# Adder convolutions: a pair of maxima added by DMA, and four channels in one written order

## The chip, the cores and the metric

The kernel runs on one core of a Trainium2 chip. The metric is device time in microseconds (us) of one execution of the whole program. The kernel before the change took 21,893.29 us in the median of three runs (21,889.71 to 21,903.57).

A core has several engines that run their own instruction lists in order and wait for each other through semaphores: TensorE (PE, matrix products into PSUM), VectorE (DVE), ScalarE (ACT), GpSimd (POOL) and SyncE (SP, which here issues DMAs). Sixteen DMA engines move data.

## The reference

The program is a chain of four layers on a tensor of 4 images, 128 channels and 64 x 64 points, all in float32: self-attention over the points (layer 0), two pairs of "shift" and "adder" convolution with batch norm (layer 1), a local attention block with an MLP (layer 2), and a selective scan (layer 3). Only layer 1 is changed. Its adder convolution is an L1 distance between each 3 x 3 patch and each output channel's weights:

```python
patches = lax.conv_general_dilated_patches(x, filter_shape=(K, K), ...)
def per_channel(wc):
    return -jnp.sum(jnp.abs(p - wc[None, :, None]), axis=1)
out = lax.map(per_channel, wf)
```

For one image and one output channel this is a sum of |p - w| over 128 input channels and 9 taps at 4096 points. There are 4 images, 128 output channels and two such convolutions: 1,024 image-channels, each with 9 taps of 128 x 4096 elements.

## The kernel before

`layer1` calls `shift_adder` twice (tags a1 and a2). The shift convolution of image b writes its result with a border of zeros into a buffer `pb` in SBUF; the adder convolution reads nine shifted views of it. Input channels lie on the 128 partitions, the 4096 points along each row.

The absolute value of a tap is made in one of two ways. ScalarE computes |p - w| directly (`absolute`, line 423, weights as the bias). VectorE computes max(p, w) (`maximum`, line 430), because |p - w| = 2 max(p, w) - p - w; the terms in p and w are put in at the end, from the sums of the window over the input channels (`sums_of_p`) and the sums of the weights (`wsum`). A third form, `plus_maximum` (line 434), adds a maximum onto a finished tile in one VectorE instruction. When it adds onto an absolute value, ScalarE has made that one with scale 0.5 (`HALF_TAP`), so the factor 2 fits both.

Each finished tile of 128 x 4096 is a *stream*: PE sums it over the partitions with eight matmuls of 512 columns (`gather`, line 381) against a vector of -1 or -2 that stands in the column of the channel (`pick`), into two PSUM banks that collect 32 output channels (a chunk). A float32 matmul has two records in the profile, so a stream has sixteen.

A channel has four activations (taps 7, 4, 5, 6), four maxima (taps 0 to 3) and one added maximum (tap 8 onto tap 7): eight streams. In every fourth channel of the first three images (`extra`) the last maximum is added onto the one before it, which leaves seven streams, and three steps of other work (`beside`) are put on PE: the window sums of this image and the shift convolution of the next. Every 32 channels `evacuate` empties the two banks.

The order of the work is that of the Python loop over channels (line 416) as the framework's scheduler lays it out. Engines run ahead as far as buffers allow: `ap` has four tiles for absolute values, `dp` three for maxima. GpSimd only clears borders (lines 84, 85 and 331), and SyncE issues all DMAs of this layer.

Of the kernel before, what the change touches and what calls it, by code (L numbers as in the profile page):

```python
# [16 lines left out]
P = 128  # L17
B = 4
# [11 lines left out]
DVE_TAPS = (0, 1, 2, 3)  # L30
ACT_TAPS = (4, 5, 6)
HALF_TAP = 7
MAX_TAP = 8
# [248 lines left out]
def shift_adder(tc, cm, load, wqs, w_add, stats, y_d, tag):  # L282
# [5 lines left out]

    nc = tc.nc
    NC = P // 32  # L290
    with ExitStack() as ctx:
# [4 lines left out]
        for t, scale in [(HALF_TAP, -0.5)] + [(t, -1.0) for t in ACT_TAPS]:  # L296
            wn[t] = cp.tile([P, P], F32, name=f"{tag}wn{t}")
            nc.vector.tensor_scalar(wn[t], wa[:, t, :], scale, None, ALU.mult)

        pick = {}  # L300
        for v in (-1.0, -2.0):
            pick[v] = cp.tile([P, 63], F32, name=f"{tag}pick{int(-v)}")
            nc.vector.memset(pick[v], 0.0)
            nc.vector.memset(pick[v][:, 31:32], v)

        xin_pool = ctx.enter_context(tc.tile_pool(name=f"{tag}x", bufs=3))
        pb_pool = ctx.enter_context(tc.tile_pool(name=f"{tag}p", bufs=2))
        dp = ctx.enter_context(tc.tile_pool(name=f"{tag}d", bufs=3))
        ap = ctx.enter_context(tc.tile_pool(name=f"{tag}a", bufs=4))
# [6 lines left out]
        sum_taps = DVE_TAPS + (MAX_TAP,)  # L316
        pw = ps_c.tile([P, NC], F32, tag="cv", name=f"{tag}pw")
        for c in range(NC):
            for g in range(4):
                for i, t in enumerate(sum_taps):  # L320
                    nc.tensor.matmul(
                        pw[32 * g : 32 * g + 32, c : c + 1], wa[:, t, 32 * c : 32 * c + 32], cm.one_col,
                        start=(i == 0), stop=(i == len(sum_taps) - 1), skip_group_check=True,
                    )
# [3 lines left out]
        def fetch(b, k):  # L328

            t = xin_pool.tile([P, RB + 2, HP], F32, tag="xin", name=f"{tag}xin{b}_{k}")  # L330
            nc.gpsimd.memset(t[:, :, 0:HP:HP - 1], 0.0)
            if k == 0:
                nc.gpsimd.memset(t[:, 0, 1 : 1 + W], 0.0)
            if k == NB - 1:
                nc.gpsimd.memset(t[:, RB + 1, 1 : 1 + W], 0.0)
            lo, hi = max(RB * k - 1, 0), min(RB * (k + 1) + 1, H)
            at = lo - (RB * k - 1)
            load(b, lo, hi, t[:, at : at + hi - lo, 1 : 1 + W])
            return t

        def convolution(b, pb):

            xin = fetch(b, 0)
            for k in range(NB):
                here, xin = xin, fetch(b, k + 1) if k < NB - 1 else None
                pc = ps_c.tile([P, BK], F32, tag="cv", name=f"{tag}pc{b}_{k}")
                for t in range(TAPS):
                    y, x = divmod(t, 3)
                    nc.tensor.matmul(
                        pc, wqs[:, t, :], here[:, y : y + RB, x : x + W],  # L350
                        start=(t == 0), stop=(t == TAPS - 1),
                    )
                    if t == TAPS - 1:
                        nc.vector.tensor_copy(pb[:, 1 + RB * k : 1 + RB * (k + 1), 1 : 1 + W], rows(pc))  # L354
                    yield

        def padded(b):
            t = pb_pool.tile([P, HP, HP], F32, tag="pb", name=f"{tag}pb{b}")
            clear_border(nc, t)
            return t  # L360

        def sums_of_p(b, pb, sp):

            for k in range(2):
                pc = ps_c.tile([P, BK], F32, tag="cv", name=f"{tag}sp{b}_{k}")
                for i, t in enumerate(sum_taps):
                    y, x = divmod(t, 3)
                    for g in range(4):
                        r = RB * (4 * k + g) + y
                        nc.tensor.matmul(  # L370
                            pc[32 * g : 32 * g + 32, :], cm.ones[:, 0:32], pb[:, r : r + RB, x : x + W],
                            start=(i == 0), stop=(i == len(sum_taps) - 1), skip_group_check=True,
                        )
                    yield
                nc.vector.tensor_copy(sp[:, k, :], pc)

        def gather(pa, jj, v, d, first=False):

            for k in range(2):
                for g in range(4):  # L380
                    nc.tensor.matmul(  # L381
                        pa[k][32 * g : 32 * g + 32, :],
                        pick[v][:, 31 - jj : 63 - jj],
                        d[:, bass.ts(4 * k + g, BK)],
                        start=first, stop=False, skip_group_check=True,
                    )

        def evacuate(b, c, pa, sp):
            for k in range(2):
                o = ep.tile([P, BK], F32, tag="ev", name=f"{tag}ev{b}_{c}_{k}")  # L390
                nc.vector.scalar_tensor_tensor(o, pa[k], wsum[:, c : c + 1], sp[:, k, :], ALU.add, ALU.add)
                nc.vector.bn_stats(stats[:, c, 2 * b + k, :], o)
                to = y_d[b, 32 * c : 32 * c + 32, :].rearrange("j (k g w) -> k g j w", k=2, g=4)
                nc.sync.dma_start(to[k], o)
# [11 lines left out]
        done, late = None, []  # L406
        for b in range(B):
            pb = pb_of[b]

            def view(t):  # L410
                y, x = divmod(t, 3)
                return pb[:, y : y + H, x : x + W]

            sp_of[b] = sp_pool.tile([P, 2, BK], F32, tag="sp", bufs=2, name=f"{tag}sps{b}")
            steps = beside(b, pb_of)
            for co in range(P):
                c, jj = divmod(co, 32)
                name = f"{tag}_{b}_{co}_"

                def absolute(t):  # L420
                    at = ap.tile([P, N], F32, tag="ab", name=f"a{name}{t}")
                    half = t == HALF_TAP
                    nc.scalar.activation(  # L423
                        rows(at), view(t), AF.Abs, bias=wn[t][:, co : co + 1], scale=0.5 if half else 1.0
                    )
                    return at

                def maximum(t):
                    dt = dp.tile([P, N], F32, tag="ad", name=f"d{name}{t}")
                    nc.vector.tensor_scalar(rows(dt), view(t), wa[:, t, co : co + 1], None, ALU.max)  # L430
                    return dt

                def plus_maximum(at, t):
                    nc.vector.scalar_tensor_tensor(  # L434
                        rows(at), view(t), wa[:, t, co : co + 1], rows(at), ALU.max, ALU.add
                    )

                if jj == 0:
                    pa = [
                        ps_a.tile([P, BK], F32, tag=f"pa{k}", name=f"{tag}pa{b}_{c}_{k}") for k in range(2)  # L440
                    ]


                extra = b < B - 1 and co % 4 == 1
                ah = absolute(HALF_TAP)
                d = maximum(DVE_TAPS[0])
                for g in late:
                    gather(*g)
                gather(pa, jj, -2.0, d, first=(jj == 0))
                if done and jj == 0:  # L450
                    evacuate(*done)
                d = maximum(DVE_TAPS[1])
                gather(pa, jj, -2.0, d)
                a = absolute(ACT_TAPS[0])
                gather(pa, jj, -1.0, a)
                a = absolute(ACT_TAPS[1])
                plus_maximum(ah, MAX_TAP)
                gather(pa, jj, -2.0, ah)
                gather(pa, jj, -1.0, a)
                if extra or b == B - 1:  # L460
                    for _ in range(3 if extra else 1):
                        next(steps, None)
                d = maximum(DVE_TAPS[2])
                if extra:
                    plus_maximum(d, DVE_TAPS[3])
                    a = absolute(ACT_TAPS[2])
                    late = [(pa, jj, -1.0, a), (pa, jj, -2.0, d)]
                else:
                    gather(pa, jj, -2.0, d)
                    a = absolute(ACT_TAPS[2])  # L470
                    d = maximum(DVE_TAPS[3])
                    gather(pa, jj, -2.0, d)
                    late = [(pa, jj, -1.0, a)]
                if jj == 31:
                    done = (b, c, pa, sp_of[b])
            for _ in steps:
                pass
        for g in late:
            gather(*g)
        evacuate(*done)  # L480


@with_exitstack
def layer1(ctx, tc, cm, w_shift1, w_add1, g1, b1, w_shift2, w_add2, g2, b2, x1d, y1d, y2d, stats_d):
# [26 lines left out]
    def plain(b, lo, hi, t):  # L511
        nc.sync.dma_start(t, rows(x1d[b])[:, lo:hi, :])

# [4 lines left out]
    def normed(b, lo, hi, t):  # L518
        nc.sync.dma_start(t, rows(y1d[b])[:, lo:hi, :])
        nc.vector.tensor_scalar(t, t, mean1, sc1, ALU.subtract, ALU.mult)  # L520
        nc.scalar.activation(t, t, AF.Relu, bias=vec["b1"])
# [872 lines left out]
```

## Time and profile before

| What | Before |
|---|---|
| median of three runs | 21,893.29 us |
| profiled execution, own time | 21,893.77 us |
| its span, first to last instruction | 21,891.9 us |
| busy: PE / DVE / ACT / POOL | 20,152.1 / 19,729.2 / 18,548.7 / 3,775.6 us |
| a1, first to last activation start | 2083.6 to 9540.2 us |
| a2, first to last activation start | 9640.0 to 17,103.6 us |
| DMA share in the adder stages | 0.01 |

The page lists groups of instructions as: line, engine, operation, output tile <- input tiles, shapes, count | busy us, mean ns of one | idle time of the engine just before them and what ended it. Records of one engine overlap slightly, and the ends of matmuls are modelled, so the distance between starts is a better measure of pace than a duration. `da` are maxima, `aa` absolute values, `a1pa` and `a2pa` the PSUM banks. In answers on one line of the code, three numbers with slashes are the minimum, median and maximum duration in ns.

### The profile page before, as it was taken

Reading aid. Unit: us, or ns where it says so; the run is one execution under the profiler, and the core shown is the slowest. Engines: PE = TensorE matmul, PEld = TensorE weight load, DVE = VectorE, ACT = ScalarE, POOL = GpSimd, SP = SyncE. Lnnn points to the kernel's source line nnn. Section 1 sums busy time; section 2 is a strip of 40 time slices with the busy share of each in tenths; the row PEclk is TensorE's granted clock in tenths of the full one; section 3 lists DMA queues with packets and bytes.
Section 4 is the critical chain, followed back from the end, with each engine's and each line's share of the span. In section 5 each row is a group of like instructions: output and inputs, shape, how many; then the busy total and the mean of one; then the engine's idle time right before and its main releaser. Section 6 shows DMA issues by size and latency. Waiting matters only on the chain.

```text
span 21891.9 us, 327596 instructions
## 1 busy us (share of the span) xinstructions
PE 20152.1 (92%) x144108; PEld 6497.4 (30%) x144108; DVE 19729.2 (90%) x9928; ACT 18548.7 (85%) x9373; POOL 3775.6 (17%) x1774
## 2 busy tenths in 40 slices
PE   9998999999999999999999999999999656779998
PEld 4443222222222232232222222222322222223333
DVE  7787999999999999989999999999999766589998
ACT  5665999999999999989999999999999422556766
POOL 5664000000000000000000000000000000179998
PEclk9999999999999999999999999999999777689999
DMA  0000000000000000000000000000000000279997
GB/s 12 13 5 14 3 4 4 3 5 4 3 4 3 4 3 2 2 8 4 4 3 4 4 4 2 4 3 3 2 2 2 33 0 5 109 224 246 254 255 220
DMA packets 279019, 811.94 MB, mean 37 GB/s; under 512 B 131212, under 2 KB 132116, under 8 KB 207444
## 3 DMA queue, kind: packets, MB, share of 16 engines
q1 hardware_dynamic: 277012, 782.60, 12.5%
q8 instruction: 1127, 18.46, 0.3%
q10 hardware_dynamic: 576, 8.39, 0.1%
q14 instruction: 304, 2.49, 0.0%
HBM read 662.02 MB, written 128.78 MB: 36 GB/s over the span
## 4 chain that ended last, share of the span: by engine, by line
ACT 29%; PE 25%; DVE 24%; issue 16%; DMA 3%; POOL 2%; SPq 1%; DVEq 0%; ACTq 0%; POOLq 0%
ACT aa L423 27%; DVE da L430 11%; PE a1pa L381 6%; PE pe L154 4%; PE pav L197 4%; PE a2pa L381 3%; DVE h L1043 3%; DVE da L434 3%; DVE aa L434 3%; DVE g L713 1%; PE mg L1058 1%; DMA du<-du_d 1%; PE pd L698 1%; POOL dbu L1022 1%; DMA dl<-delta_d 1%
## 5 line engine op out<-in xcount | busy, mean ns | idle before, releaser
L423 ACT ACTIVATE aa<-a1pb,a1wn 128x4096 f32<-128x4096 f32 x2048 | 7411.6, 3711 | 179.2 <-DVE a1pb L354 130.5
L423 ACT ACTIVATE aa<-a2pb,a2wn 128x4096 f32<-128x4096 f32 x2048 | 7410.6, 3712 | 45.4 <-PE a2pa L381 41.5
L430 DVE TENSOR_SCALAR da<-a2pb,a2wa 128x4096 f32<-128x4096 f32 x1952 | 4470.3, 2347 | 0.2
L430 DVE TENSOR_SCALAR da<-a1pb,a1wa 128x4096 f32<-128x4096 f32 x1952 | 4469.5, 2347 | 0.7 <-PE a1pa L381 0.6
L381 PE MATMUL a2pa<-da,a2pick 128*32 128x512 f32 x31232 | 3617.3, 594 | 254.8 <-DVE da L430 252.0
L381 PE MATMUL a1pa<-da,a1pick 128*32 128x512 f32 x31232 | 3615.2, 594 | 253.5 <-DVE da L430 250.8
L381 PE MATMUL a2pa<-aa,a2pick 128*32 128x512 f32 x32768 | 3714.1, 593 | 4.8 <-ACT aa L423 3.3
L381 PE MATMUL a1pa<-aa,a1pick 128*32 128x512 f32 x32768 | 3712.5, 592 | 4.9 <-ACT aa L423 3.3
L434 DVE SCALAR_TENSOR_TENSOR aa<-a1pb,a1wa,aa 128x4096 f32<-128x4096 f32 x512 | 2295.1, 4483 | 282.2 <-ACT aa L423 278.0
L434 DVE SCALAR_TENSOR_TENSOR aa<-a2pb,a2wa,aa 128x4096 f32<-128x4096 f32 x512 | 2295.2, 4483 | 278.3 <-ACT aa L423 274.7
L1058 PE MATMUL mg<-h,ident 128*128 128x512 f32 x4096 | 1955.7, 615 | 204.4 <-ACT m L1067 168.6
L1043 DVE TENSOR_TENSOR_SCAN h<-da,h,dbu 128x1024 f32<-128x1024 f32 x768 | 1804.4, 2350 | 125.6 <-ACT da L1029 35.9
L381 PEld LDWEIGHTS a2pa<-aa,a2pick 128*32 128x32 f32 x32768 | 1069.1, 110 | 2464.8 <-issue 2397.0
L381 PEld LDWEIGHTS a1pa<-aa,a1pick 128*32 128x32 f32 x32768 | 1068.9, 110 | 2463.4 <-issue 2400.0
L381 PEld LDWEIGHTS a2pa<-da,a2pick 128*32 128x32 f32 x31232 | 987.3, 110 | 2706.9 <-issue 2053.2
L381 PEld LDWEIGHTS a1pa<-da,a1pick 128*32 128x32 f32 x31232 | 987.3, 110 | 2704.8 <-issue 2053.9
L191 POOL TENSOR_TENSOR ssum<-ssum,et 128x512 f32<-128x512 f32 x960 | 1228.8, 1280 | 233.4 <-ACT et L186 166.6
L1022 POOL TENSOR_TENSOR dbu<-du,B 128x2048 f32<-128x2048 f32 x256 | 1157.1, 4533 | 104.1 <-DMA du<-du_d 49.6
L1071 POOL TENSOR_TENSOR m<-m,C 128x2048 f32<-128x2048 f32 x256 | 1156.6, 4529 | 93.5 <-ACT m L1067 79.9
L1058 PEld LDWEIGHTS mg<-h,ident 128*128 128x128 f32 x4096 | 724.7, 191 | 1437.7 <-ACT m L1067 699.2
L156 ACT COPY et<-pe 128x512 f32<-128x512 f32 x1024 | 595.5, 582 | 592.2 <-PE pe L154 575.4
L154 PE MATMUL pe<-q,k 128*128 128x512 f32 x2048 | 1051.1, 596 | 8.7 <-DVE mx L164 8.1
(273 smaller groups left out, 13587.0 us busy)
## 6 DMA issues: line engine op xcount, KB each, us to landing
dl<-delta_d SPq DMA_DIRECT2D x256, 512.0 KB
dl<-delta_d SPq DMA_DIRECT2D x512, 256.0 KB
du<-du_d SPq DMA_DIRECT2D x256, 512.0 KB
du<-du_d SPq DMA_DIRECT2D x512, 256.0 KB
xs_d<-xs SPq DMA_DIRECT2D x8, 2048.0 KB
sz_d<-sz SPq DMA_DIRECT2D x64, 256.0 KB
delta_d<-dv SPq DMA_DIRECT2D x32, 512.0 KB
du_d<-du SPq DMA_DIRECT2D x32, 512.0 KB
```

Source lines behind the costliest of these rows:

```text
L154: nc.tensor.matmul(pe, k[:, bass.ts(j, P)], unit[u, "q"], start=True, stop=True)
L156: nc.scalar.copy(et, pe)
L191: nc.gpsimd.tensor_tensor(unit[u, "sum"], unit[u, "sum"], at, ALU.add)
L197: nc.tensor.matmul(unit[u, "av"], image[u // NB][2][:, j, :], at, start=(j == 0), stop=(j == NJ - 1))
L381: nc.tensor.matmul(pa[k][32 * g : 32 * g + 32, :], pick[v][:, 31 - jj : 63 - jj], d[:, bass.ts(4 * k + g, BK)], start=first, stop=False, s ...
L423: nc.scalar.activation(rows(at), view(t), AF.Abs, bias=wn[t][:, co : co + 1], scale=0.5 if half else 1.0)
L430: nc.vector.tensor_scalar(rows(dt), view(t), wa[:, t, co : co + 1], None, ALU.max)
L434: nc.vector.scalar_tensor_tensor(rows(at), view(t), wa[:, t, co : co + 1], rows(at), ALU.max, ALU.add)
L1022: then(nc.gpsimd.tensor_tensor(t, du, by_states(tiles[n][0], 0, h), ALU.mult))
L1043: then(nc.vector.tensor_tensor_scan(t[:, cols][:, s], da[:, s], st[n, "dbu", h][:, cols][:, s], 0.0 if e % 4 == 0 else st["last"], ALU.mul ...
L1058: then(nc.tensor.matmul(pm, cm.ident, st[n, way, h][:, bass.ts(k, BK)], start=(way == 0), stop=(way == 1)))
L1071: then(nc.gpsimd.tensor_tensor(m, m, by_states(tiles[n][0], 1, h), ALU.mult))
```

## The change

Four consecutive channels become one pattern with three kinds of channel.

- In every channel taps 0 and 1 are a *pair*: VectorE makes both maxima in two halves of 2048 points, and a DMA on GpSimd's queue adds one onto the other in SBUF (`accum_op=ALU.add`). The half sums are half streams; together the two halves are one stream.
- Channel 0 of four: three more maxima (taps 2, 3, 4) and four absolute values (5 to 8).
- Channels 1 and 3: two more maxima (2, 3), four absolute values, and tap 4 added onto one of them, made with scale 0.5.
- Channel 2: four more maxima (2 to 5), three absolute values (6 to 8).

That is 8, 7, 8 and 7 streams. For four channels: 15 activations, 11 full maxima, 16 half maxima, 2 added maxima, 8 adding DMAs of 1 MB and 30 streams. Tap 5 is a maximum only in channel 2 of four, so its part of the window sums and weight sums is taken through `third` and `w_third`, which hold ones and weights in those channels alone; the window sums now have six taps.

The order is written out as a string, `ORDER`, for four channels; the number ahead of a letter is the channel (-1 is the last channel of the four before). Capital letters make something (P pair, M maximum, A absolute value, S added maximum), the same letters small sum it on PE, and C stands for three steps of the other work and the evacuation. `keep_in_program_order` pins every instruction of the stage on its engine's list to that order. Absolute values get three buffers, full maxima two, half maxima six. The shift convolution fetches its input two blocks ahead instead of one.

```diff
-DVE_TAPS = (0, 1, 2, 3)
-ACT_TAPS = (4, 5, 6)
-HALF_TAP = 7
-MAX_TAP = 8
+PAIR_TAPS = (0, 1)
+MAX_TAPS = (2, 3, 4, 5)
+ADDED_TAP = 4
+ABS_TAPS = {0: (5, 6, 7, 8), 1: (5, 6, 7, 8), 2: (6, 7, 8), 3: (5, 6, 7, 8)}
+HALF = {1: 2, 3: 1}
+ORDER = """
+    -1p0 0P0 -1m0 0M0 0a0 0A2 0M1 0a1 -1p1 0A3 0m0 0P1 0m1 0M2 1A0 0a2 0a3 1P1 1M1 1A1 0m2 0p0 1a0 1P0
+    1A2 1m1 1M0 0p1 1a1 1A3 1S2 1m0 1p1 2A0 1a3 2M2 1a2 2M3 1p0 2A1 2m2 2M0 2a0 2A2 2m3 2a1 2P0 3A0 2M1
+    2m0 2a2 3A1 2P1 2m1 3a0 3P0 3A2 3S1 3C0 3A3 2p0 3a2 3P1 3a1 3M1 2p1 4A0 3a3 3M0 3m1 4A1
+""".split()
...
-        dp = ctx.enter_context(tc.tile_pool(name=f"{tag}d", bufs=3))
-        ap = ctx.enter_context(tc.tile_pool(name=f"{tag}a", bufs=4))
+        mp = ctx.enter_context(tc.tile_pool(name=f"{tag}m", bufs=6))
+        dp = ctx.enter_context(tc.tile_pool(name=f"{tag}d", bufs=2))
+        ap = ctx.enter_context(tc.tile_pool(name=f"{tag}a", bufs=3))
...
+        def pair(n, h):
+            ms = []
+            for t in PAIR_TAPS:
+                mt = mp.tile([P, HL], F32, tag="am", name=f"m{tag}_{n}_{t}_{h}")
+                v = view(n, t, h * H // 2, (h + 1) * H // 2)
+                then(nc.vector.tensor_scalar(rows(mt), v, weight(n, t), None, ALU.max))
+                ms.append(mt)
+            then(nc.gpsimd.dma_start(ms[1], ms[0], accum_op=ALU.add))
+            streams[n, "p", h] = (-2.0, ms[1], (h,))
...
+        for n in range(0, B * P, 4):
+            b, co = divmod(n, P)
+            if co == 0:
+                sp_of[b] = sp_pool.tile([P, 2, BK], F32, tag="sp", bufs=2, name=f"{tag}sps{b}")
+                steps = beside(b, pb_of)
+            for at, kind, i in map(parsed, ORDER):
+                m = n + at
+                if kind == "C":
+                    for _ in range(3):
+                        next(steps, None)
...
+                elif kind in make:
+                    if m < B * P:
+                        begin(m, kind, i)
+                else:
+                    summed(m, kind, i)
```

## The prediction

> **What bounds the kernel now.** I read the page first for where the time lies, then busy time by stretch, then the order in time inside one stretch, because shares over the whole span mix stages. The page's group list puts the two adder convolutions (a1, a2) on top:
>
> ```profile
> span 21891.9 us, 327596 instructions
> ...
> L423 ACT ACTIVATE aa<-a1pb,a1wn 128x4096 f32<-128x4096 f32 x2048 | 7411.6, 3711 | 179.2 <-DVE a1pb L354 130.5
> ...
> L430 DVE TENSOR_SCALAR da<-a2pb,a2wa 128x4096 f32<-128x4096 f32 x1952 | 4470.3, 2347 | 0.2
> ...
> L381 PE MATMUL a2pa<-da,a2pick 128*32 128x512 f32 x31232 | 3617.3, 594 | 254.8 <-DVE da L430 252.0
> ...
> L434 DVE SCALAR_TENSOR_TENSOR aa<-a1pb,a1wa,aa 128x4096 f32<-128x4096 f32 x512 | 2295.1, 4483 | 282.2 <-ACT aa L423 278.0
> ```
>
> By line 423's own answer a1 runs from 2083.6 to 9540.2 us and a2 from 9640.0 to 17103.6 (starts of the first and last activation). With the last one's 3.7 us that is 7460 and 7467 us for 512 image-channels each: 14.57 and 14.58 us a channel, 1,024 channels, 68% of the span. Two stretches of 500 us inside a1 (columns: stretch, length, then busy us and instructions of each engine, clock, DMA share, GB/s):
>
> ```profile
> 5900.00:6400.00 500.00, 482.68 (x4306) 145.74 (x4302) 486.05 (x179) 496.51 (x138) 0.26 (x2) 1.00 0.01 4
> 6400.00:6900.00 500.00, 485.82 (x4312) 143.27 (x4308) 483.73 (x179) 495.90 (x138) 0.25 (x2) 1.00 0.01 4
> ```
>
> ScalarE (fourth busy figure) is at 99%; PE and VectorE at 97%. ScalarE sets the pace and the others are close behind. Record durations overlap a little, so I take intervals between starts from the timeline:
>
> ```profile
> 5999.80 36.19 ACT L423 ACTIVATE aa<-a1pb,a1wn 128x4096 f32<-128x4096 f32 x10
> 6000.71 9.13 DVE L430 TENSOR_SCALAR da<-a1pb,a1wa 128x4096 f32<-128x4096 f32 x4
> 6004.85 5.33 PE L381 MATMUL a1pa<-aa,a1pick 128*32 128x512 f32 x48
> 6010.00 3.62 PE L381 MATMUL a1pa<-da,a1pick 128*32 128x512 f32 x32
> ```
>
> Activation: (36.19-3.71)/9 = 3.61 us. Maximum: (9.13-2.35)/3 = 2.26. Added maximum: 4.39 (start 6021.95, next start 6026.34). PE: 5.15 us from start to start over 48 records = 0.107 us, and a stream has 8 matmuls of two records, so 1.72 us. A half-size maximum (128x2048) exists elsewhere, line 711 at 1284 ns mean, so an interval near 1.20.
>
> [...]
>
> ```profile
> L212 DVE TENSOR_SCALAR o<-o,bv,g x32: 536/1580/1586, 158.1 to 1978.3; 128x512 f32<-128x512 f32 x32
> ...
> L331 POOL MEMSET a1xin<- x32: 123/126/3117, 2009.2 to 6902.7; 128x20 f32 x32
> ```
>
> (minimum/median/maximum ns). L212 took 0.54 us with GpSimd idle and 1.58 when a GpSimd addition of 1.26 us had begun with it. The GpSimd memset of 126 ns took 3.12 us once: it began at 5376.56 inside the first of two back-to-back maxima (5374.99 to 5379.60) and ended only after the second. Back-to-back maxima do not let GpSimd in between; inside an added maximum (two SBUF inputs) memsets took their 0.13 us.
>
> **The change, part by part, for four channels.**
> ScalarE: 16 activations become 15: 15 x 3.61 = 54.2 us, 13.54 a channel (before 14.44, and 14.57 measured: 0.13 above its floor).
> PE: 31.25 streams on average (7.75 a channel in three images, 8 in the last) become 30: 30 x 1.72 / 4 = 12.88, plus the next image's convolution, 144 records of about 0.47 us over 128 channels = 0.54, plus the window sums, now six taps, 96 x 0.107/128 = 0.08. Sum 13.50 (before 14.0).
> VectorE: 11 maxima x 2.26 = 24.9; 16 half maxima x 1.20 = 19.2; 2 added maxima x 4.39 = 8.8; 52.9/4 = 13.22, plus evacuations and copies, about 0.12: 13.34 (before about 13.95).
> GpSimd and DMA, new: eight additions of 1 MB each. A row of 8 KB is one packet, and the shortest 8 KB packets in the trace took 0.309 us; eight rows an engine read twice are 4.9 us, 8 x 4.9 = 39.6 us of a period near 55: 72% of DMA engines that are at 1% now. [...] What hides it: between a pair's making and its sum the written order puts 8.5, 6.5, 6, 6, 4, 4.5, 5 and 7 PE streams, the three of 4 to 5 with 2.8 us of convolution as well: 9.7 to 14.6 us, and 6.9 where no convolution is left (the last image). The six half buffers hold three pairs, and the shortest stretch of VectorE work before a pair's buffer returns is about 11 us. [...] beyond it PE waits, its queue is in order, and all later streams wait, then the two buffers of the full maxima, then VectorE.
> Fetches two ahead, other constants, `third`: some tens of small operations a layer, at nothing. They lie beside the same stream work; uncovered they are a few us.
>
> Sum: the floors are 13.54, 13.50, 13.34. The old excess was 0.13 with the next engine 0.4 behind; with three engines within 0.2 us and one fixed order I take 0.20: 13.74, 0.83 less than 14.57. Times 1,024 = 850. The profiled execution's own time is 21,893.8 us (span 21,891.9) and the median of runs 21,893.3, so both give **21,045 us**.
>
> The unknown is the descriptor writing. Lower bound nothing (Pool is idle, 0.26 us busy in 500). Upper bound: a lock held as by a GpSimd addition, 1.27 us, eight times, would put VectorE at 13.34 + 2 x 1.27 = 15.9. I take at most 0.2 us each, which VectorE's slack absorbs, and keep both ends.
>
> **Rivals.**
> *Part of the gain*: GpSimd gets in, holding VectorE 0.3 to 0.5 us a DMA. VectorE then has 13.94 to 14.34 plus 0.1: 21,390 to 21,800. For it: L212. Equal to before at about 0.6 us a DMA.
> *Slower[...]*: from the second half pair of the fourth channel (3P1) to 1M0 stand twelve tokens, five pairs and seven full maxima[...]: 5 x 2.4 + 7 x 2.26 = 27.8 us. If they run back to back, the descriptors of pairs made early in that stretch wait as the memset did, past the 10 to 14 us of cover. PE then stops, buffers fill, VectorE stops, and only then GpSimd gets in. [...] It decides from 3.3 us exposed per four channels (4 x 0.83). Against it: semaphore waits break such stretches, and a gap is all GpSimd needs.
> *Slower, through the DMA's rate*: eight transfers must fit in 58 us to equal before, 7.3 us each. At 8.2 us (2 MB of reads at the 255 GB/s of the scan stage) the DMA alone needs 16.4 us a channel: 23,770. Against it: 131,212 of the span's 279,019 packets are under 512 B, and these are 8 KB.
> *No change*: gain and stalls cancel, 21,850 to 21,940. That the edit is not made is excluded: the built program has 1,920 activations a layer where it had 2,048, and 1,024 adding DMAs.
>
> **How the numbers follow.** Likeliest, cover holds: 0.45, between 20,900 (excess 0.06) and 21,250. Part of the gain, to 21,850: 0.13. Cancelled: 0.03. [...] 0.39 in all, of which about 0.22 below 22,900. The range 20,900 to 22,900 leaves out 0.17 above and 0.03 below. Within 0.2%, about what a measurement tells from none, counts as same.
>
> **What would show it.** Right: ScalarE again at 98 to 99% in a1, one channel per 13.7 us, PE's waits on the pair's DMA short, half maxima at 1.28 us, landings under 10 us. [...] half or full maxima lengthened beyond 2.35, or VectorE idle on DMA semaphores and PE on pair streams, landings of 12 us and more with long GpSimd waits. Rate: DMA share near 1 in these stages. What would make me wrong: descriptors that cannot be written under maxima, or adding rows slower than two reads.

## The result and the profile after

The changed kernel takes 21,815.2 us in the median of seven runs (21,793.3 to 21,843.5), the kernel before 21,894.9 beside it: a ratio of 0.9964, 95% interval 0.9952 to 0.9976. It is faster by 80 us, 0.4%, where 850 were forecast. The profiled execution answers as follows. First the page: the span, the chain that ended last, groups of instructions (busy us, mean ns | idle time ahead of the group and what ended it), and the DMA's time to landing.

```profile
span 21809.7 us, 323448 instructions
...
DMA ma<-ma 26%; PE a2pa L424 11%; PE a1pa L424 11%; DVE ma L478 7%; DVE da L469 6%; PE pe L163 4%; PE pav L206 4%; DVE h L1092 3%; DVE g L762 1%; DMA du<-du_d 1%; PE mg L1107 1%; PE pd L747 1%; DMA dl<-delta_d 1%; POOL dbu L1071 1%; DVE aa L461 1%
...
L455 ACT ACTIVATE aa<-a1pb,a1wn 128x4096 f32<-128x4096 f32 x1920 | 6987.3, 3713 | 567.2 <-PE a1pa L424 431.0
...
L469 DVE TENSOR_SCALAR da<-a1pb,a1wa 128x4096 f32<-128x4096 f32 x1408 | 3275.0, 2348 | 293.1 <-PE a1pa L424 292.6
...
L478 DVE TENSOR_SCALAR ma<-a1pb,a1wa 128x2048 f32<-128x2048 f32 x2048 | 2545.0, 1280 | 267.8 <-DMA ma<-ma 266.4
...
L424 PE MATMUL a1pa<-ma,a1pick 128*32 128x512 f32 x8192 | 1090.7, 605 | 334.0 <-DMA ma<-ma 331.7
...
ma<-ma POOLq DMA_DIRECT2D x2048, 1024.0 KB, 9.3
```

The instructions have the durations that the prediction gave them: maxima 2348 ns, half maxima 1280 ns, neither lengthened. What is new is idle time on every engine of these stages, and one cause at its head: PE waits for the adding DMA ahead of the pair sums, ScalarE and full maxima wait for PE (their buffers), and half maxima wait for the DMA (theirs). The DMA heads the chain, with 26% of the span.

The same two stretches of a1 as before the change (length, then busy us of PE, weight loads, VectorE, ScalarE, GpSimd; clock, DMA share, GB/s):

```profile
5900.00:6400.00 500.00, 474.41 (x4216) 137.32 (x4212) 459.60 (x257) 469.64 (x130) 122.71 (x75) 1.00 0.73 146
6400.00:6900.00 500.00, 477.56 (x4216) 139.74 (x4209) 462.23 (x257) 470.35 (x130) 124.65 (x71) 1.00 0.73 147
```

ScalarE fell from 99% to 94%: nobody is at the bound. By the first and last activation, a1 runs from 2086.1 to 9503.9 us and a2 from 9611.8 to 17,021.4, which with the last activation's 3.7 us is 14.50 and 14.48 us a channel, in place of 14.57 and 14.58 before and 13.74 forecast. The line that issues the adding DMAs (duration of GpSimd's instruction, who waited for the DMA, time to landing):

```profile
L480 POOL DMA_DIRECT2D ma<-ma x2048: 859/1947/12477, 2088.6 to 17026.9; - x187
...
who waited for it (us, times):
  PEld a1pa L424: 743.7, 553
  PEld a2pa L424: 728.8, 576
  DVE ma L478: 527.5, 445
  PE a1pa L424: 331.7, 322
  PE a2pa L424: 305.5, 297
...
DMA to landing us min/median/max: 7.0/9.3/18.6
```

A DMA has landed when the last update of its semaphore has come. From the records of single semaphore updates and matmuls in the first three images of a1, for the eight pairs of four channels (medians, us): the landing, counted from the end of the pair's second maximum on VectorE, and the cover, the time from that point to the pair's sum on PE where nothing makes it wait. The cover is measured in e3 below, which has the same order and hardly ever a late DMA.

| pair | 0P0 | 0P1 | 1P1 | 1P0 | 2P0 | 2P1 | 3P0 | 3P1 |
|---|---|---|---|---|---|---|---|---|
| landing | 8.9 | 9.2 | 9.9 | 9.6 | 8.5 | 9.2 | 13.1 | 10.0 |
| cover | 13.2 | 10.6 | 10.2 | 9.9 | 9.9 | 9.6 | 11.5 | 10.7 |

Four of the eight have at most 0.7 us to spare, and 3P0 has less than nothing: it is made right behind 2P1 and its rows queue behind that transfer (they begin 4.8 us after the end of its issue, and 2P1's after 1.0). From the start of the last matmul ahead to the start of a pair's sum PE takes 0.79 us on average, where 0.41 is usual. Over the 2,048 sums of both layers the excess is 789 us. That is the gain that is missing (21,815 less the 21,032 of e1: 783). Of the 789 us, 772 fall on 760 sums that start within 0.06 us of the landing of their own DMA, so this loss is waiting for the landing. It is larger where the cover is smaller: 282 us fall on the last images of the two layers, a quarter of the channels, where no convolution lies between a pair and its sum.

### The profile page after: what moved, and what is told of

It is laid out like the page before. It is cut to its first block, busy times and chain, and to the rows that moved or that the text cites. A ratio compares the mean times of both kernels' runs of the same rounds, so it can differ in the third digit from the quotient of the medians.

```text
span 21809.7 us, 323448 instructions
## 1 busy us (share of the span) xinstructions
PE 19720.1 (90%) x139180; PEld 6260.6 (29%) x139180; DVE 19100.0 (88%) x12244; ACT 17694.9 (81%) x9117; POOL 7447.8 (34%) x3822
## 4 chain that ended last, share of the span: by engine, by line
PE 37%; DMA 29%; DVE 22%; issue 7%; POOL 2%; ACT 2%; SPq 0%; DVEq 0%; POOLq 0%; ACTq 0%
DMA ma<-ma 26%; PE a2pa L424 11%; PE a1pa L424 11%; DVE ma L478 7%; DVE da L469 6%; PE pe L163 4%; PE pav L206 4%; DVE h L1092 3%; DVE g L762 1%; DMA du<-du_d 1%; PE mg L1107 1%; PE pd L747 1%; DMA dl<-delta_d 1%; POOL dbu L1071 1%; DVE aa L461 1%
## 5 line engine op out<-in xcount | busy, mean ns | idle before, releaser
L480 POOL DMA_DIRECT2D ma<-ma x2048 | 3693.6, 1804 | 11187.1 <-DVE ma L478 7337.7
L455 ACT ACTIVATE aa<-a2pb,a2wn 128x4096 f32<-128x4096 f32 x1920 | 6979.3, 3711 | 349.9 <-PE a2pa L424 333.0
L469 DVE TENSOR_SCALAR da<-a1pb,a1wa 128x4096 f32<-128x4096 f32 x1408 | 3275.0, 2348 | 293.1 <-PE a1pa L424 292.6
L469 DVE TENSOR_SCALAR da<-a2pb,a2wa 128x4096 f32<-128x4096 f32 x1408 | 3275.3, 2349 | 274.0 <-PE a2pa L424 273.3
L478 DVE TENSOR_SCALAR ma<-a1pb,a1wa 128x2048 f32<-128x2048 f32 x2048 | 2545.0, 1280 | 267.8 <-DMA ma<-ma 266.4
L478 DVE TENSOR_SCALAR ma<-a2pb,a2wa 128x2048 f32<-128x2048 f32 x2048 | 2545.6, 1280 | 262.3 <-DMA ma<-ma 261.1
L424 PE MATMUL a1pa<-da,a1pick 128*32 128x512 f32 x22528 | 2677.9, 597 | 88.2 <-DVE da L469 86.8
L424 PE MATMUL a2pa<-da,a2pick 128*32 128x512 f32 x22528 | 2671.5, 596 | 81.0 <-DVE da L469 79.9
L424 PE MATMUL a1pa<-ma,a1pick 128*32 128x512 f32 x8192 | 1090.7, 605 | 334.0 <-DMA ma<-ma 331.7
L424 PE MATMUL a2pa<-ma,a2pick 128*32 128x512 f32 x8192 | 1089.0, 604 | 307.7 <-DMA ma<-ma 305.5
L200 POOL TENSOR_TENSOR ssum<-ssum,et 128x512 f32<-128x512 f32 x960 | 1228.9, 1280 | 233.4 <-ACT et L195 166.5
```

Source lines behind the costliest of these rows:

```text
L200: nc.gpsimd.tensor_tensor(unit[u, "sum"], unit[u, "sum"], at, ALU.add)
L424: then(nc.tensor.matmul(pa[k][32 * g : 32 * g + 32, :], pick[v][:, 31 - jj : 63 - jj], d[:, bass.ts(4 * at + g, BK)], start=(n // 32, k) n ...
L455: then(nc.scalar.activation(rows(at), view(n, t), AF.Abs, bias=bias, scale=scale))
L469: then(nc.vector.tensor_scalar(rows(dt), view(n, t), weight(n, t), None, ALU.max))
L478: then(nc.vector.tensor_scalar(rows(mt), v, weight(n, t), None, ALU.max))
L480: then(nc.gpsimd.dma_start(ms[1], ms[0], accum_op=ALU.add))
```

## The experiments

Theory L: the written order reaches a pair's sum before its DMA has landed, so cover and landing decide. The rivals: the written order or the small pools cost the time by themselves (O), the transfer's traffic costs it (D), and VectorE's maxima hold GpSimd off while it issues a DMA (P). Medians are beside 21,893 to 21,899 us of the kernel before; "long" are GpSimd issues over 3 us, of 2,048; the landing in this table is counted from the start of the issue. The maxima hold GpSimd off in the traces (a memset of 0.13 us took 3.12 before the change, an issue up to 12.48 us in it); the added maximum and the openings below read two tiles in SBUF, and are called "two-input". What the prediction and the expectations call writing descriptors is, in the traces, the instruction with which GpSimd issues a DMA, 1.95 us in the median of the change; what it does in that time, and why maxima hold it off, no run shows.

| run | us | us a channel, a1 / a2 | long | landing, median us |
|---|---|---|---|---|
| the change | 21,815 | 14.50 / 14.48 | 11 | 9.3 |
| e1 no DMA | 21,032 | 13.67 / 13.78 | | |
| e2 short rows | 22,461 | 15.13 / 15.13 | 219 | 4.3 |
| e3 copies by SyncE | 21,081 | 13.72 / 13.83 | | 7.0 |
| e4 later sums, seven halves | 21,178 | 13.73 / 13.98 | 31 | 9.8 |
| e5 seven halves | 23,189 | 15.70 / 15.99 | 227 | 10.3 |
| e6 later sums | 22,115 | 14.77 / 14.80 | 138 | 9.6 |
| e7 short rows, 3S1 moved | 21,672 | 14.37 / 14.38 | 249 | 4.3 |
| e8 as e4, 3S1 moved | 22,473 | 15.17 / 15.09 | 191 | 12.2 |
| e9 as e5, with openings | 21,730 | 14.39 / 14.40 | 11 | 9.6 |
| e10 as e6, with openings | 21,531 | 14.20 / 14.22 | 5 | 9.2 |
| e11 openings alone | 21,847 | 14.50 / 14.53 | 6 | 9.2 |
| e12 as e4, with openings | 21,140 | 13.76 / 13.88 | 18 | 9.7 |
| e13 plain copy, openings | 21,095 | 13.74 / 13.84 | 13 | 6.1 |
| e14 as e2, with openings | 21,079 | 13.73 / 13.83 | 13 | 4.5 |

**e1: no adding DMA.** Tap 0's maxima are made and not summed.

```diff
-            then(nc.gpsimd.dma_start(ms[1], ms[0], accum_op=ALU.add))
```

> The changed kernel without the adding DMA: the pair's second maximum alone is summed, so the first maximum of each pair is left out of the result; VectorE, ScalarE and PE do the same work in the same order. Theory L (the landing of the pair comes later than PE wants it, and nothing else costs): one channel per 13.7 us where the changed kernel has 14.5, total 20,950 to 21,100 us, PE idle before pair sums gone, ScalarE at 98%. Rival O (the fixed order and the smaller pools, three absolute values and two maxima, cost the gain by themselves): 14.4 to 14.5 us a channel, 21,700 to 21,820 us. Rival P (writing descriptors beside VectorE costs): also near 21,000 here.

Ratio 0.9604 (0.9585 to 0.9624). The first of the two stretches:

```profile
5900.00:6400.00 500.00, 498.07 (x4451) 150.95 (x4444) 488.86 (x275) 497.99 (x138) 0.38 (x3) 1.00 0.02 4
```

PE and ScalarE are at 99.6%, VectorE at 97.8%. The floors stand, and O falls: order and pools cost nothing when no sum waits for a DMA.

**e2: short rows.** Only 512 of 2,048 columns are added, the rest of tap 0 is left out.

```diff
-            then(nc.gpsimd.dma_start(ms[1], ms[0], accum_op=ALU.add))
+            then(nc.gpsimd.dma_start(ms[1][:, 0:BK], ms[0][:, 0:BK], accum_op=ALU.add))
```

> The changed kernel with DMAs that add only 512 of the 2048 columns; the addition of the other columns is left out. As many DMAs, as many rows and descriptors, rows a quarter as long. Theory L: rows of 2 KB take about 0.16 us, so eight rows take 1.3 us and not 5.15; a landing takes about 5.4 us and not 9.3, PE hardly waits, total 20,950 to 21,150 us. Rival P: [...] the time stays at 21,700 to 21,820 us. Rival O: the same, 21,700 to 21,820.

Ratio 1.0257 (1.0236 to 1.0278): a landing of less than half the length, and a slower kernel, which no theory had expected; all the expected ranges miss. The issues of one position, 3P1, had become long, mostly 12.47 us, so this run didn't test L and D, and P came up.

**e3: the same reads by SyncE.** Two plain copies from SyncE's queue stand in for the addition; tap 1's maxima are overwritten. The two layers' shift weights share one tile, to make room for the scratch tile; this edit is in e4 to e6, e8 to e10 and e12 too.

```diff
-            then(nc.gpsimd.dma_start(ms[1], ms[0], accum_op=ALU.add))
+            scr = scp.tile([P, HL], F32, tag="scr", name=f"r{tag}_{n}_{h}")
+            then(nc.sync.dma_start(scr, ms[0]))
+            then(nc.sync.dma_start(ms[1], ms[0]))
```

> Each adding DMA is replaced by two plain copies of 1 MB on SyncE's queue, one into a scratch tile and one onto the second maximum, so that as many bytes are read as by the addition; the addition is left out. [...] (One weight tile serves both convolutions, to make room for the scratch tile; about 12 us.) Theory L[...]: what goes is 0.9 to 2.1 us of descriptor writing; landings about 7.5 us, total 21,000 to 21,300 us. Theory L with the transfer alone too long: landings stay near 9 us, total 21,600 us and more. Rival O: 21,700 to 21,820 us.

Ratio 0.9627 (0.9607 to 0.9646), at a DMA share of 0.77 in the stretch from 5900 to 6400 us, more than the 0.73 of the change. D falls: that much traffic by itself costs 50 us against e1 at most. From the end of its maxima a pair lands after 8.0 us in the median (6.3 at 2P0 to 10.6 at 3P0), and 91 of 2,048 sums start right at the landing (760 in the change). Landing and time are near what theory L with GpSimd's instruction as a part of the landing had expected, 7.5 us and 21,000 to 21,300. GpSimd's instruction and the addition are both gone, so this run doesn't part them; e13 does.

**e4: later sums and seven half buffers.** Each pair's sum comes one stream later in the order; the other tokens stay.

```diff
-    -1p0 0P0 -1m0 0M0
+    0P0 -1m0 -1p0 0M0
...
-        mp = ctx.enter_context(tc.tile_pool(name=f"{tag}m", bufs=6))
+        mp = ctx.enter_context(tc.tile_pool(name=f"{tag}m", bufs=7))
```

> The whole computation. Each pair's sum stands one stream later in the written order, and the half maxima have seven buffers instead of six (one weight tile serves both convolutions, to make room). Landing, descriptors and transfers are as in the changed kernel. Theory L: 1.7 us more cover is enough for the median pair, PE's waits on pairs nearly go, one channel per 13.7 us, total 20,980 to 21,200 us. Rival P and rival O: no cover helps, 21,700 to 21,830 us.

Ratio 0.9674 (0.9658 to 0.969). The landing is no shorter (9.8 us), but it comes 1.2 to 5.5 us before the sum, by the medians of the eight pairs in a1. This is L's positive test, and it beats both kernels.

**e5 and e6: each half of e4 alone.** e5 has the seven buffers, e6 the later sums.

> Edit: seven half buffers in place of six, in the written order of the change; the shift weights of both layers share one tile to make room. Theory L (a pair's sum is reached before its DMA has landed): a seventh buffer lets VectorE start a pair earlier by up to one stream, but the sum stands where it stood, so a part of the stalls goes: about 14.0 to 14.3 us a channel, 21,300 to 21,650. If the buffers alone had been the fault: 13.75, as with both edits, 21,180. If they do nothing: 14.49, 21,815.

> Edit: each pair's sum is written one stream later, with six half buffers as in the change. Theory L: the sum waits less, but a half buffer is held one stream longer, so VectorE's next pair comes later and part of the gain is handed back: 14.0 to 14.3 us a channel, 21,300 to 21,650. If the order alone had been the fault: 13.75, 21,180. If the buffers take everything back: 14.49, 21,815.

Ratios 1.0592 (1.0576 to 1.0608) and 1.0103 (1.0086 to 1.012): both expectations miss, and both kernels are slower than the kernel before. In e5 one stretch of the timeline, all engines, shows why (start, length, engine, instruction, count, and in brackets the idle time ahead):

```profile
6030.27 2.47 DVE L475 TENSOR_SCALAR ma<-a1pb,a1wa 128x2048 f32<-128x2048 f32 x2
...
6032.66 4.61 DVE L466 TENSOR_SCALAR da<-a1pb,a1wa 128x4096 f32<-128x4096 f32 x2
...
6033.03 13.67 POOL L477 DMA_DIRECT2D ma<-ma  x1 [5.69 <-DVE ma L475]
...
6037.18 2.47 DVE L475 TENSOR_SCALAR ma<-a1pb,a1wa 128x2048 f32<-128x2048 f32 x2
...
6039.57 4.61 DVE L466 TENSOR_SCALAR da<-a1pb,a1wa 128x4096 f32<-128x4096 f32 x2
...
6044.10 2.48 DVE L475 TENSOR_SCALAR ma<-a1pb,a1wa 128x2048 f32<-128x2048 f32 x2
```

The pair made at 6030.27 is 3P1. GpSimd begins to issue its DMA at 6033.03, when the next maximum has begun, and is done at 6046.70; VectorE ran maxima back to back until 6046.58. PE's own timeline in the same place:

```profile
6040.30 3.62 PE L421 MATMUL a1pa<-aa,a1pick 128*32 128x512 f32 x32
6052.95 1.93 PE L421 MATMUL a1pa<-ma,a1pick 128*32 128x512 f32 x8 [9.04 <-DMA ma<-ma]
6054.66 5.74 PE L421 MATMUL a1pa<-da,a1pick 128*32 128x512 f32 x32
6060.23 3.61 PE L421 MATMUL a1pa<-aa,a1pick 128*32 128x512 f32 x32
```

PE stood still for 9.04 us until the DMA had landed, and VectorE stopped, for 11.79 us, because PE no longer emptied its buffers. So the DMA waits here for a pause of VectorE, and VectorE pauses only once PE has stopped for want of the DMA. The issue ends 0.12 us behind VectorE's last maximum (6046.70 less 6046.58), and was held off over eight maxima. Over the change and the runs without openings, 1,016 of 1,066 long issues end within 0.14 us behind a VectorE instruction that a pause or a two-input instruction follows. In e6 it is no circle: 137 of its 138 long issues, at 2P0 and mostly of 6.6 us, end where an added maximum follows.

**e7 and e8: a two-input step behind 3P1.** The added maximum 3S1 moves to right behind 3P1, on the short rows (e7) and on e4 (e8).

```diff
-    3S1 3C0 3A3 2p0 3a2 3P1 3a1 3M1
+    3C0 3A3 2p0 3a2 3P1 3S1 3M1
...
-    3m1 4A1
+    3a1 3m1 4A1
```

> Edit: the DMA adds only 512 of the 2048 columns, as in the run with short rows (the rest of tap 0's maxima is left out), and two tokens move: the added maximum 3S1 from before 3C0 to right after 3P1, and its sum 3a1 to just before 3m1. Theory P (with short rows the kernel was slow because the descriptors of 3P1 were locked out for 12.47 us by a row of back-to-back maxima): the added maximum behind 3P1 lets GpSimd write, its issues at 3P1 fall to 2 us or so, and the time falls from 22,461 to 21,050 to 21,200. If something else made the short rows slow: 22,400 to 22,500, with the waits at another place.

> Edit: later sums and seven half buffers as in the run before of that name, and 3S1 moved to right after 3P1 with its sum moved to just before 3m1. The whole computation is done. Theory P: the 22 long GpSimd issues of that run, 18 of them in a2, go, and a2 comes from 13.98 to about 13.75 us a channel, 120 us at most: 21,060 to 21,180. If those long issues cost nothing or the moved steps cost ScalarE its place: 21,180 to 21,300.

At 3P1 the issue took 0.86 us in both, as expected. But the long issues came back at 0P0: 249 in e7, mostly 10.2 us, and 191 in e8, mostly 13.7 us. e7 came down to 21,672 (0.99; 0.9885 to 0.9915), more than half of the way, and 0P0 has the longer cover (13.2 against 10.7 us); e8 went from 21,178 to 22,473 (1.0266; 1.025 to 1.0281). Both times miss what was expected: mending one place moves the lock-out.

**e9 to e12: openings for all pairs.** Behind the first maximum that follows a pair stands a two-input instruction of 0.22 us whose output nobody uses; 3P0, which an added maximum follows, needs none.

```diff
+        def opening():
+            if due.pop():
+                then(nc.vector.scalar_tensor_tensor(
+                    scr, wa[:, 0, 0:8], wa[:, 0, 0:1], wa[:, 1, 0:8], ALU.max, ALU.add
+                ))
+            due.append(0)
```

> Edit: seven half buffers, and a VectorE instruction of another form (one addition with two SBUF inputs, 128x8, its output unused) behind the first maximum that follows each pair. Theory P (the run with seven half buffers lost 1,374 us against the change because GpSimd's issue at 3P1 was locked out for 9 to 13.7 us, 223 times, by back-to-back maxima): the opening lets GpSimd in at the next boundary, issues over 3 us all but vanish, and the time falls from 23,189 to 21,200 to 21,750, the upper part of it if sums ahead of their landing (theory L) still cost as much as in the change. If 128x8 is too short to let GpSimd in, or something else made it slow: about 23,100 to 23,300.

> Edit: each pair's sum one stream later with six half buffers, and the same openings. Theory P (that run's 137 issues of 6.6 us at 2P0 set its time): they vanish, and the time falls from 22,115 to 21,200 to 21,600, by theory L because a half buffer is held one stream longer. If the openings let nobody in: about 22,100.

> Edit: the change as it is, with the same openings. The change has only 11 issues over 3 us, 76 us in all, so theory P has little to win here: 21,740 to 21,830. Theory L (the sums come before the landing) says the same. The openings themselves cost VectorE two short instructions a channel, some 0.1 to 0.2 us: if VectorE has no room for them, up to 21,980.

> Edit: later sums, seven half buffers, and the same openings; the whole computation is done. Theory P: the 31 issues over 3 us (237 us in all, of which a part was behind other work) go: 21,080 to 21,170, both layers at about 13.75 us a channel. If the openings cost VectorE its slack: 21,180 to 21,350.

Ratios 0.9922 (0.9907 to 0.9937), 0.9834 (0.9819 to 0.9848), 0.9977 (0.997 to 0.9984) and 0.9656 (0.9642 to 0.9671). e9, e10 and e12 are where P and L put them. e11 is 17 us above its 21,740 to 21,830, in the stretch given for openings that cost VectorE time. Between e5 and e9 the openings are the only edit, and 1,460 us go. No run has an opening in the form of a maximum, so it isn't shown that the form counts, and not just one more instruction at that place. The line of e9 that issues the DMAs:

```profile
L490 POOL DMA_DIRECT2D ma<-ma x2048: 852/1855/7187, 2074.0 to 16931.4; - x187
```

With the lock-outs away, four runs part what L says: neither edit 21,847, seven halves 21,730, later sums 21,531, both 21,140. Later sums alone take PE's wait ahead of the pair sums in a1 from 312.9 us (e11) to 31.1 (e10), but they hold each half buffer longer, and VectorE's wait for the DMA ahead of its half maxima goes up from 201.4 us in e11 to 287.1 in e10:

```profile
L487 DVE TENSOR_SCALAR ma<-a1pb,a1wa 128x2048 f32<-128x2048 f32 x2048 | 2561.8, 1282 | 287.1 <-DMA ma<-ma 285.0
```

In e12 both waits are gone; first the groups, then the stretch:

```profile
L487 DVE TENSOR_SCALAR ma<-a1pb,a1wa 128x2048 f32<-128x2048 f32 x2048 | 2538.9, 1281 | 10.6 <-DMA ma<-ma 10.0
...
L421 PE MATMUL a1pa<-ma,a1pick 128*32 128x512 f32 x8192 | 1070.9, 595 | 34.7 <-DMA ma<-ma 34.4
```

```profile
5900.00:6400.00 500.00, 496.70 (x4434) 150.01 (x4430) 494.27 (x334) 494.93 (x138) 125.25 (x76) 1.00 0.78 157
```

PE, VectorE and ScalarE are all at 99%. e12 is a version to use in place of the change: 755 us below the kernel before and 675 below the changed one. Its interval overlaps that of e4, so what the openings add to e4 is not settled; e4 has 31 long issues and e12 has 18.

**e13 and e14: which term of the landing.** e13 is e11 with a plain copy from GpSimd's queue (tap 1's maxima are overwritten); e14 is e2 with openings.

```diff
-            then(nc.gpsimd.dma_start(ms[1], ms[0], accum_op=ALU.add))
+            then(nc.gpsimd.dma_start(ms[1], ms[0]))
```

> Edit: in the change, GpSimd's DMA copies tap 0's half maxima over tap 1's in place of adding them (tap 1's maxima are thus left out), with the openings and with the written order and the six half buffers of the change. [...] only the second read of each row goes. Theory L: the landing falls from 9.2 us to about 6.5 (8 rows of 0.31 in place of 0.64), under the 9.6 to 13 us between a pair's making and its sum, so the sums no longer wait: 13.75 to 13.9 us a channel, 21,050 to 21,200. If what costs is GpSimd's writing of descriptors beside the maxima and not the landing's length: as with the openings alone, 21,750 to 21,850.

> Edit: the run with short rows (512 of 2048 columns added, the rest of tap 0 left out), with the openings. Theory P (lock-outs alone made short rows slow; moving the added maximum only moved them from 3P1 to 0P0): issues over 3 us all but vanish, 13.7 to 13.85 us a channel, 21,050 to 21,150. If short rows are slow for another reason: 21,600 to 22,450.

Ratios 0.9632 (0.9616 to 0.9648) and 0.9627 (0.9612 to 0.9641). In e13's answer the issue is nearly as long as in the change (1.84 us against 1.95), and the landing is 3.2 us shorter:

```profile
L491 POOL DMA_DIRECT2D ma<-ma x2048: 527/1840/6565, 2088.8 to 16309.5; - x187
...
DMA to landing us min/median/max: 4.4/6.1/10.7
```

So GpSimd's instruction beside the maxima costs little by itself (e13 is 14 us above e3); it costs as a part of a landing that exceeds the cover. Taking 3.2 us off the landing was enough. e14 settles e2: with the lock-outs gone the short rows are fast, so these had made them slow.

## Why the prediction was wrong

*The floors and the excess (13.54, 13.50, 13.34, sum 13.74)* were right: e1 has 13.67 and 13.78 us a channel, and e13, with GpSimd's DMAs, 13.74 and 13.84.

*The half maxima and the DMA's rate* were right: 1280 ns; an adding row took 0.644 us where two reads at 0.309 gave 0.618; the DMA share is 0.73 where 72% was worked out.

*The descriptor writing* is the step that failed: "I take at most 0.2 us each, which VectorE's slack absorbs." It was priced as time taken from VectorE. VectorE gave none. It was GpSimd that waited: from finished maxima to the end of its instruction are 2.4 us in the median, of which the instruction is 1.95 (0.86 at 3P0, where an added maximum runs beside it). From there to the landing are 7.5 us; by the medians of the first three images of a1, 0.9 us pass to the first row, 5.7 over the rows, where the prediction reckoned 4.9, and 0.35 behind the last. For what a landing takes beside its rows the prediction had only its author's estimate. So the landing was 2.4 + 7.5 us, and what cover there was to spare was used up. The upper bound, 1.27 us, was near the 1.1 us that GpSimd lost beside the maxima (1.95 less 0.86), but was put on the wrong engine.

*The cover, 9.7 to 14.6 us*, was right as far as it went: 9.6 to 13.2 measured in e3. Two things were left out. Two transfers can follow each other at once: 3P0 is made 2.4 us after 2P1, its rows wait for the other's 5.5 us, and it lands after 13.1. And for the last image the prediction itself had only 6.9 us of cover, and put the wait there at nothing; e3 has 7.0 us of cover there at 2P0.

*The six buffers* counted as harmless; they were the second tie. Even with later sums they hold back 390 us (e10 against e12).

*What would show it*: landings under 10 us did come about, in the median, and were no proof. The figure to ask for was landing less cover, pair by pair.

*The rivals.* Part of the gain came near as a size and not as a mechanism (VectorE held): 21,815 against its 21,390 to 21,800, a sum that with its own "plus 0.1" gives 21,350 to 21,760. That the time lies between 20,900 and 22,900 is owed to the width of that range, which takes in slower kernels too. The rival in which GpSimd is held off, 0.28 of the forecast (0.11 went to the DMA's rate), was told with its right place for the change, e2 and e5 (3P1; in e6 it was 2P0, in e7 and e8 0P0), and its right circle (PE stops, buffers fill, VectorE stops, GpSimd gets in). In the change it struck 11 times of 2,048, but e2, e5, e6, e7 and e8 show how near it lay: 138 to 249 times, and up to 23,189 us. The rival of the DMA's rate fell with e3. "Back-to-back maxima do not let GpSimd in between" was read from one memset and is too general, as the last section shows.

## What to carry to other kernels

Price a DMA that GpSimd issues by its time from the data's being ready to its landing, with GpSimd's instruction beside VectorE's maxima in it (here 2.4 of 9.9 us), and set it against the cover of each consumer, one by one; a median that fits hides the ones that don't. Cover is made with two edits at once, a later consumer and a buffer for what it holds longer; here each alone gave 0.5% to 1.4% with openings and both gave 3.2%. Where VectorE runs maxima back to back, a two-input instruction of 0.22 us behind each point where GpSimd must issue kept the wait from closing into a circle here: 227 long issues in e5, 11 in e9.

## What the runs showed of the hardware

- GpSimd can stay locked out over a whole row of back-to-back maxima, 13.67 us in e5. But it also gets in at the boundary of two such maxima, without lengthening either: 1,054 of the 2,048 issues of the change ended so, after 1.85 to 2.09 us. In e6 one position, 2P0, with the same VectorE instructions behind it and starts within some 20 ns, took 6.6 us in most of 137 issues and about 1.84 us in most of the other 119. What decides it stays open.
- A shorter transfer made the kernel slower (e2: 22,461 us with 219 long issues; with openings, e14, 21,079 with 13). In the changed kernel VectorE often pauses for PE or a DMA, and I read these stalls as part of what lets GpSimd in there; no run shows that by itself.
- One long pause of PE cost twice. After 9.04 us of idling in e5, 32 matmul records took 5.74 us where 3.61 is usual: the granted clock was 0.50 from 6053 to 6057 us and 1.00 again from 6059. How short a pause is enough, no run here shows.
